# Probabilities transposed on VectorE in 32-row blocks, and V multiplied in eight tiles of 32 rows and 64 columns

## The chip, the cores and the metric

One core of a Trainium2 chip runs the whole kernel. The metric is the device time of one launch in microseconds. The kernel before was timed three times: 888.75, 889.93 and 890.03 us, median 889.93 us.

## What is computed

A block of two layers on x of 4 batches x 1024 tokens x 256 features, in fp32. The first is a gated cross attention to a short context (64 rows per batch, 16 heads of 64), the second a mixture of experts (8 experts, the best two per token, each 256 to 1024 to 256).

```python
qh = jnp.einsum('bld,hdk->hblk', q, w_qs)          # q = layernorm(x)
kh = jnp.einsum('bld,hdk->hblk', k, w_ks)          # k = v = context
vh = jnp.einsum('bld,hdk->hblk', v, w_vs)
attn = jax.nn.softmax(jnp.einsum('hblk,hbmk->hblm', qh, kh), axis=-1)
out = jnp.einsum('hblm,hbmk->hblk', attn, vh) * qh  # the output is gated by the query
...
x = x + jnp.tanh(g_xattn[0]) * (out @ w_proj.T + b_proj)
x = x + jnp.tanh(g_ffn[0]) * ffn(layernorm(x))      # 8 experts, top 2
```

## The kernel before, in words

The 4096 tokens are cut into eight groups g of 512, each of four tiles t of 128 (`T`, `G`, `NG`, lines 68 to 70). Two groups share a batch. The 16 heads are handled as eight pairs (`NP`), and the pairs as two halves of four: `halves` (L359) makes two buffers, `qT` and `aT` are each such a pair of buffers with features or context rows on the partitions and the 512 tokens of the group along them.

The main loop (L1109) runs g from 0 to 10 and t from 0 to 3. I call one g a stage. A stage does, for tile t of group g:

- `probabilities` (L381): eight score products per tile into the two-bank PSUM tile `sc` (pool `ps2`, two buffers, L100), then row maximum (L394), subtraction (L396) on VectorE, exponential on ScalarE (L399), row sum (L401) and reciprocal (L402) on VectorE, and the product with the reciprocal on GpSimd (L404). The result `pr` has tokens on the partitions.
- `transpose_probabilities` (L408), one tile behind: eight TensorE transposes (L414) into two PSUM banks `pa`, each copied by ScalarE into `aT` (L415).
- `queries` (L366) for the next group: per pair two products (L370) into a bank, copied by ScalarE (L377).
- `attend` (L419), for the group before, in four steps q at t = 1: per step two banks `po`, four products of 64 rows and 64 columns with 512 tokens streaming (L428), then two VectorE products (L437) that multiply the bank into `qT` in place. Between the steps stand the query products of the loop.
- `project` (L439), for the group before, at t = 2 and 3: 32 products (L445) per call, and one VectorE operation (L452) that adds the result to x.
- two groups behind: layernorm for the second layer (`ln_norm`, L266; transposes L281, copies L286), router logits (L467, copies L475 and L479), and every second stage `route` (L483) and `place` (L528).

`values` (L333) makes V in stage 0 and ScalarE copies it into `vs` in four pieces per bank (L352). All one-bank PSUM tiles, those of `pq`, `pa`, `po`, `pp`, `pt`, `pl`, come from one pool of four buffers, `ps1` (L101, `bank` L106). Large SBUF blocks come from three shared sets: "group" (8), "weight" (7) and "hidden" (2) (L93). The expert weights of the second layer take "weight" blocks as they come free. From stage 6 on, the experts' slots (`run_slots`, L994: gather, L899, L978, scatter) run between the attention's steps, and from about 440 us they are alone.

The text gives the order in which work is offered; the framework's scheduler then orders each engine's queue by priority and by what it takes to be ready, assigns the buffers and places the semaphores. Every engine works through its queue in that order. `keep_in_program_order` and `issue_after` pin a few instructions.

A hardware matmul record is half an fp32 product: every L370, L385, L428, L445 product appears as two MATMUL records, a transpose (L281, L414) as one.

Of the kernel before, what the change touches and what calls it, by code (L numbers as in the profile page):

```python
# [15 lines left out]
P = 128  # L16
# [5 lines left out]
def kernel(  # L22
# [14 lines left out]
    out: bass.AP,  # L37
):


# [81 lines left out]
    dram = ctx.enter_context(tc.tile_pool(name="dram", bufs=1, space=bass.MemoryType.DRAM))  # L122
    normed = dram.tile([N, D], F32, tag="normed", name="normed")
    lists = dram.tile([E * N + BEHIND, 2], I32, tag="lists", name="lists")
    outf = out.rearrange("b l d -> (b l) d")
# [64 lines left out]
    kT = [keys_of[b // 2][:, b % 2] for b in range(B)]  # L190
    vs = block([P, B, NP, DK], "vs", "weight")

# [140 lines left out]
    def values(ctxT):  # L333

        n = 512 // P
        for b0 in range(0, B, 2):
            for p0 in range(0, NP, n):
                pv = bank(f"pv_{b0}_{p0}")
                for c in range(NC):
                    nc.tensor.matmul(  # L340
                        pv,
                        ctxT[:, c, b0 * M : (b0 + 2) * M],
                        wv[:, c, p0 * P : (p0 + n) * P],
                        start=(c == 0),
                        stop=(c == NC - 1),
                    )
                pvv = pv.rearrange("p (q j r k) -> p q j r k", j=2, r=2, k=DK)
                q0 = p0 // 2
                for i in range(2):
                    to = vs[:, b0 + i].rearrange("p (q r) k -> p q r k", r=2)  # L350
                    for j in range(2):
                        nc.scalar.copy(  # L352
                            to[j * M : (j + 1) * M, q0 : q0 + n // 2],
                            pvv[i * M : (i + 1) * M, :, j],
                        )
                yield


    def halves(name, share="group"):  # L359

        return [block([P, NP // 2, G], f"{name}_{i}", share) for i in range(2)]

    def of_pair(t, p):
# [17 lines left out]
    def probabilities(g, t, qT):  # L381

        sc = ps2.tile([P, NP // 2, 2, 2, M], F32, tag="ps2", name=f"sc_{g}_{t}")
        for p in range(NP):
            nc.tensor.matmul(  # L385
                sc[:, p // 2, :, p % 2, :],
                of_pair(qT, p)[:, t * P : (t + 1) * P],
                kT[g // GB][:, p, :],
                start=True,
                stop=True,  # L390
            )
        scv = sc.rearrange("p q r j m -> p (q r j) m")
        mx = small.tile([P, H], F32, tag="mx", name=f"mx_{g}_{t}")
# [14 lines left out]
    def transpose_probabilities(g, t, pr, aT):  # L408
        prv = pr.rearrange("p (i j) m -> p i (j m)", j=2)
        n = 512 // P  # L410
        for p0 in range(0, NP, n):
            pt = bank(f"pa_{g}_{t}_{p0}")
            for i in range(n):
                nc.tensor.transpose(pt[:, i * P : (i + 1) * P], prv[:, p0 + i, :], ident)  # L414
            nc.scalar.copy(  # L415
                aT[p0 // n][:, :, t * P : (t + 1) * P], pt.rearrange("p (i q) -> p i q", i=n)
            )

    def attend(g, q, qT, aT):  # L419

        po = [bank(f"po_{g}_{2 * q + j}") for j in range(2)]
        for r in range(2):
            for j in range(2):
                half = slice(j * M, (j + 1) * M)
                i = q * 2 + r
                nc.tensor.matmul(  # L428
                    po[j][r * DK : (r + 1) * DK],
                    vs[half, g // GB, i, :],  # L430
                    of_pair(aT, i)[half],
                    start=True,
                    stop=True,
                )
        for j in range(2):
            own = of_pair(qT, 2 * q + j)
            nc.vector.tensor_tensor(own, po[j], own, ALU.mult)  # L437

# [670 lines left out]
    for g in range(NG + 3):  # L1109
        attention_ends = g >= NG  # L1110
        if g < NG:
            qT, aT = qTs[g], halves(f"aT_{g}", "hidden" if g % 2 and g + 1 < NG else "group")
            held[g] = (qT, aT)
# [4 lines left out]
        ends = before_last % GB == GB - 1 and before_last >= 0  # L1118
        for t in range(T):
            if g < NG:  # L1120
                pr = probabilities(g, t, qT)
# [4 lines left out]
            products = [(h, p) for h, pairs in parts[g].items() for p in pairs[t]]  # L1126
            if 0 < g <= NG and t == 1:
                for q in range(NP // 2):
                    attend(g - 1, q, *held[g - 1])
                    for h, p in products[q : q + 1]:  # L1130
                        queries(h, qTs[h], [p])
                products = products[NP // 2 :]
            for h, p in products:
# [4 lines left out]
            if g == 0:  # L1138
                for _ in range(value_parts[t]):
                    next(pending_values)  # L1140
            if 0 <= before_last < NG and t < 2:
                norm_again(before_last, t)
# [72 lines left out]
```

## Time and profile before

| what | value |
|---|---|
| median of three runs | 889.93 us |
| the profiled execution, its own time | 918.12 us |
| its span in the trace | 916.3 us |
| mean granted TensorE clock | 0.986 |
| TensorE busy (matmul) | 871.4 us, 95% of the span |
| VectorE busy | 327.8 us, 36% |
| ScalarE busy | 263.9 us, 29% |
| GpSimd busy | 403.0 us, 44% |
| L414 transposes of probabilities, x256 | 33.5 us busy |
| L428 products with V, x256 | 37.2 us busy |
| L437 VectorE products after them, x64 | 40.3 us busy |
| L415 ScalarE copies of transposes, x64 | 34.6 us busy |
| scores of tile 1 start in stages 1 to 7 | 74.9, 117.4, 164.0, 212.5, 260.2, 308.9, 351.0 us |

The profile gives, for one execution, each engine's busy time, the instructions by source line, what each one waited for and the chain of work that ended last. A busy time of matmuls is a union of records whose ends are modelled, so a TensorE that is 95% busy is not one at 95% of its peak; what counts is the distance from one start to the next. A mean in nanoseconds is the length of one record, which for matmuls overlaps its neighbours.

### The profile page before, as it was taken

The numbers are of one execution on the slowest core, as the hardware profiler recorded it, in microseconds if no ns is written. First come the engines' busy times: TensorE is split into PE (matmuls) and PEld (weight loads), VectorE is DVE, ScalarE is ACT, GpSimd is POOL, SyncE is SP. The second block draws the span as 40 slices with busy tenths as digits, with TensorE's granted clock in tenths as the row PEclk, the third lists the DMA queues.
The fourth block names the chain that finished last, engine by engine and source line by source line (L and its number), as shares of the span: only waits on it lengthen the run. The fifth ranks groups of instructions, "written<-read, shape, count | busy, mean of one in ns | idle before, by whom it ended". The sixth has DMA issues, their size and how long they took to land.

```text
span 916.3 us, 11723 instructions
## 1 busy us (share of the span) xinstructions
PE 871.4 (95%) x4328; PEld 657.5 (72%) x4328; DVE 327.8 (36%) x729; ACT 263.9 (29%) x414; POOL 403.0 (44%) x392
## 2 busy tenths in 40 slices
PE   8999999999999998997997899999999999999995
PEld 5556858574857576865885787777777777888884
DVE  3467585777468748631155300000000001100010
ACT  4653353425242425432140121211211211121110
POOL 2051212146213553065447565555455555564443
PEclk9999999999999999998998899999999999999998
DMA  9600000001010225276372575744444564457111
GB/s 203 195 1 1 24 24 24 24 19 30 1 46 1 47 90 188 72 141 143 115 262 63 143 248 166 237 149 140 148 140 142 176 198 148 135 188 267 51 36 42
DMA packets 85279, 102.33 MB, mean 112 GB/s; under 512 B 29366, under 2 KB 71740, under 8 KB 85216
## 3 DMA queue, kind: packets, MB, share of 16 engines
q1 hardware_dynamic: 62656, 66.96, 24.4%
q0 software_dynamic: 11600, 25.25, 8.8%
q10 hardware_dynamic: 10960, 9.31, 3.7%
q8 instruction: 36, 0.59, 0.3%
q14 instruction: 27, 0.22, 0.1%
HBM read 84.75 MB, written 17.33 MB: 111 GB/s over the span
## 4 chain that ended last, share of the span: by engine, by line
PE 80%; DVE 10%; another core or an unknown queue 3%; issue 3%; DMA 1%; POOL 1%; ACT 1%; POOLq 0%; ACTq 0%; DVEq 0%
PE py L978 23%; PE ph L899 22%; PE pp L445 11%; PE pq L370 10%; PE sc L385 5%; PE pa L414 2%; PE pt L867 2%; PE po L428 2%; DVE qT L437 1%; PE pk L317 1%; DVE sm L401 1%; DVE pr L396 1%; DVE mx L394 1%; PE pt_b L281 1%
## 5 line engine op out<-in xcount | busy, mean ns | idle before, releaser
L978 PE MATMUL py<-w,hT 128*128 128x256 f32 (+1 forms) x1168 | 238.3, 369 | 9.2 <-issue 8.7
L899 PE MATMUL ph<-xT,w 128*128 128x256 f32 (+2 forms) x896 | 233.8, 418 | 2.1 <-ACT xT L872 1.2
L978 PEld LDWEIGHTS py<-w,hT 128*128 128x128 f32 (+1 forms) x1168 | 199.8, 184 | 40.2 <-issue 14.0
L899 PEld LDWEIGHTS ph<-xT,w 128*128 128x128 f32 x896 | 170.0, 191 | 57.5 <-issue 1.6
L907 ACT ACTIVATE hT<-ph 128x1024 f32<-128x1024 f32 (+3 forms) x84 | 69.9, 835 | 370.6 <-PE ph L899 319.5
L966 DVE TENSOR_SCALAR x<-py,ids 128x256 f32<-128x256 f32 (+1 forms) x72 | 33.5, 465 | 381.9 <-PE py L978 348.3
L404 POOL TENSOR_TENSOR pr<-pr,sm 128x1024 f32<-128x1024 f32 x32 | 60.9, 1902 | 218.1 <-DVE sm L402 202.1
L370 PE MATMUL pq<-nT_a,wq 128*128 128x512 f32 x256 | 117.0, 597 | 0.4 <-issue 0.2
L445 PE MATMUL pp<-wp,qT 128*128 128x256 f32 x512 | 113.2, 379 | 0.0
L445 PEld LDWEIGHTS pp<-wp,qT 128*128 128x128 f32 x512 | 97.0, 190 | 18.2 <-issue 5.3
L922 POOL DMA_INDIRECT x<-out_dram,ids x68 | 69.3, 1018 | 81.7 <-DMA out_dram<-x,ids 61.9
L845 POOL DMA_INDIRECT x<-normed,ids x68 | 67.9, 999 | 53.4 <-DMA ids<-lists 34.3
L970 POOL TENSOR_TENSOR x<-x,x 128x256 f32<-128x256 f32 (+1 forms) x67 | 48.3, 721 | 90.5 <-DVE x L966 77.8
L370 PEld LDWEIGHTS pq<-nT_a,wq 128*128 128x128 f32 x256 | 45.9, 190 | 53.5 <-issue 47.6
L939 POOL DMA_INDIRECT out_dram<-x,ids x68 | 69.0, 1015 | 23.2 <-POOL x L970 18.0
L568 POOL DMA_INDIRECT lists<-entry,to_row x64 | 62.1, 971 | 20.5 <-issue 17.9
L385 PEld LDWEIGHTS sc<-keys,qT 128*128 128x128 f32 x512 | 62.9, 192 | 7.9 <-issue 7.5
L385 PE MATMUL sc<-keys,qT 128*128 128x128 f32 x512 | 67.4, 278 | 0.0
L415 ACT COPY aT<-pa 128x512 f32<-128x512 f32 x64 | 34.6, 590 | 91.2 <-PE pa L414 71.1
L394 DVE TENSOR_REDUCE mx<-sc 128x16 f32<-128x1024 f32 x32 | 39.0, 1220 | 29.5 <-PE sc L385 28.3
L401 DVE TENSOR_REDUCE sm<-pr 128x16 f32<-128x1024 f32 x32 | 38.9, 1215 | 20.9 <-ACT pr L399 20.9
L377 ACT COPY qT<-pq 128x512 f32<-128x512 f32 x64 | 35.7, 582 | 28.4 <-PE pq L370 28.4
(209 smaller groups left out, 624.8 us busy)
## 6 DMA issues: line engine op xcount, KB each, us to landing
w<-in_L_ffn_w_dram SPq DMA_DIRECT2D x56, 1024.0 KB
out_dram<-x ACTq DMA_DIRECT2D x8, 512.0 KB
normed<-keep_b ACTq DMA_DIRECT2D x8, 512.0 KB
x<-in_x_dram SPq DMA_DIRECT2D x7, 512.0 KB
x<-normed,ids POOLq DMA_INDIRECT x68
x<-out_dram,ids POOLq DMA_INDIRECT x68
out_dram<-x,ids POOLq DMA_INDIRECT x68
wq<-in_L_xattn_w_qs_dram SPq DMA_DIRECT2D x4, 256.0 KB
```

Source lines behind the costliest of these rows:

```text
L370: nc.tensor.matmul(pq, wq[:, c, p * P : (p + 1) * P], nT[g][:, c, :], start=(c == 0), stop=(c == NC - 1),)
L385: nc.tensor.matmul(sc[:, p // 2, :, p % 2, :], of_pair(qT, p)[:, t * P : (t + 1) * P], kT[g // GB][:, p, :], start=True, stop=True,)
L404: nc.gpsimd.tensor_tensor(pr, pr, sm.unsqueeze(2).to_broadcast([P, H, M]), ALU.mult).ins
L445: nc.tensor.matmul(pp[:, i, :], of_pair(qT, p)[:, t * P : (t + 1) * P], wp[:, p, :], start=(p == 0), stop=(p == NP - 1),)
L568: nc.gpsimd.indirect_dma_start(out=lists, out_offset=bass.IndirectOffsetOnAxis(ap=to_row[:, k, i : i + 1], axis=0), in_=entry[:, k, i, :], ...
L845: gather = nc.gpsimd.indirect_dma_start(out=xin[t][:n], out_offset=None, in_=normed[: tokens_of(s)], in_offset=bass.IndirectOffsetOnAxis(a ...
L899: nc.tensor.matmul(ph[:, i, :], a[:, c, f * P : (f + 1) * P], xT[:, c, :], start=(c == 0), stop=(c == NC - 1),)
L907: nc.scalar.activation(hT[f0 // per_tile][:, f1 : f1 + step, :], ph, AF.Silu)
L922: gather = nc.gpsimd.indirect_dma_start(out=acc[t][:r], out_offset=None, in_=outf[:n], in_offset=bass.IndirectOffsetOnAxis(ap=ids[:r, t, 0 ...
L939: put = nc.gpsimd.indirect_dma_start(out=outf[:n], out_offset=bass.IndirectOffsetOnAxis(ap=ids[:r, t, 0:1], axis=0), in_=acc[t][:r], in_of ...
L970: nc.gpsimd.tensor_tensor(acc[t][:r], acc[t][:r], y[t][:r], ALU.add)
L978: nc.tensor.matmul(py[t][rows], hT[f // per_tile][:, f % per_tile, t * P : t * P + r], b[:, f, columns], start=(f == 0), stop=(f == NF - 1),)
```

## The change

V is not copied into `vs` any more. One copy per bank brings it into a block `made`, two DMAs write it to DRAM, and `load_values` reads each batch's V back into a block of its own, with the 64 context rows cut into two halves of 32 and each half repeated on the four quarters of the partitions (eight DMAs per batch, on SyncE's queue). The score tile is laid out pair by pair. The probabilities are transposed by VectorE, in blocks of 32 by 32, two instructions per tile; the four token quarters of a tile so come to lie on the four quarters of the partitions. `attend` is called twice per group, for half the pairs at a time, at t = 1 and t = 2 and ahead of `probabilities` there. It takes all four banks of `ps1` at once, one for each token quarter, and runs 64 products of 32 rows and 64 columns with 128 tokens streaming, two accumulating into each place; then four VectorE products.

```diff
     def values(ctxT):
...
+        made = block([P, B // 2, H * DK], "values", "weight")
...
-                        nc.scalar.copy(
-                            to[j * M : (j + 1) * M, q0 : q0 + n // 2],
-                            pvv[i * M : (i + 1) * M, :, j],
-                        )
+                nc.scalar.copy(made[:, b0 // 2, p0 * P : (p0 + n) * P], pv)
                 yield
+            nc.sync.dma_start(v_dram[b0 * M : (b0 + 2) * M, :], made[:, b0 // 2])
+
+    def load_values(b):
+
+        v_of[b] = block([P, M // U, H, DK], f"v_{b}", "weight")
+        for m in range(M // U):
+            rows = v_dram[b * M + m * U : b * M + (m + 1) * U, :].rearrange("m (h k) -> m h k", k=DK)
+            for a in range(T):
+                nc.sync.dma_start(v_of[b][a * U : (a + 1) * U, m], rows)
...
+    def for_probabilities(name, share):
+
+        return [block([P, T, NP * M // U, U], f"{name}_{i}", share) for i in range(2)]
...
     def transpose_probabilities(g, t, pr, aT):
-        prv = pr.rearrange("p (i j) m -> p i (j m)", j=2)
-        n = 512 // P
-        for p0 in range(0, NP, n):
-            pt = bank(f"pa_{g}_{t}_{p0}")
-            for i in range(n):
-                nc.tensor.transpose(pt[:, i * P : (i + 1) * P], prv[:, p0 + i, :], ident)
-            nc.scalar.copy(
-                aT[p0 // n][:, :, t * P : (t + 1) * P], pt.rearrange("p (i q) -> p i q", i=n)
+
+        n = H * M // 2
+        for h in range(2):
+            nc.vector.transpose(
+                aT[h][:, t], pr.rearrange("p h m -> p (h m)")[:, h * n : (h + 1) * n].rearrange("p (b u) -> p b u", u=U)
             )
...
-    def attend(g, q, qT, aT):
...
-        po = [bank(f"po_{g}_{2 * q + j}") for j in range(2)]
-        for r in range(2):
-            for j in range(2):
...
+    def attend(g, h, qT, aT):
+
+
+        po = [bank(f"po_{g}_{h}_{a}") for a in range(T)]
+        for i in range(NP // 2):
+            for m in range(M // U):
+                for r in range(2):
+                    for a in range(T):
+                        quarter = slice(a * U, (a + 1) * U)
+                        nc.tensor.matmul(
+                            po[a][r * DK : (r + 1) * DK, i * T * U : (i + 1) * T * U],
+                            v_of[g // GB][quarter, m, h * NP + 2 * i + r, :],
+                            aT[h][quarter, :, (2 * i + r) * (M // U) + m, :],
+                            start=(m == 0),
+                            stop=(m == M // U - 1),
+                        )
+        own = qT[h].rearrange("p i (t a u) -> p a i t u", t=T, u=U)
+        for a in range(T):
+            nc.vector.tensor_tensor(
+                own[:, a], po[a].rearrange("p (i t u) -> p i t u", t=T, u=U), own[:, a], ALU.mult
+            )
...
         for t in range(T):
+            if 0 < g <= NG and t in (1, 2):
+                attend(g - 1, t - 1, *held[g - 1])
             if g < NG:
                 pr = probabilities(g, t, qT)
...
-            if 0 < g <= NG and t == 1:
-                for q in range(NP // 2):
-                    attend(g - 1, q, *held[g - 1])
-                    for h, p in products[q : q + 1]:
-                        queries(h, qTs[h], [p])
-                products = products[NP // 2 :]
...
+            if (g, t) == (0, T - 1):
+                load_values(0)
+                load_values(1)
+            elif g % GB == GB - 1 and g > GB - 1 and g // GB + 1 < B and t == 0:
+                load_values(g // GB + 1)
```

More of the change, by code (lines that the diff above doesn't have):

```diff
@@ L123 @@
     normed = dram.tile([N, D], F32, tag="normed", name="normed")
+    v_dram = dram.tile([B * M, H * DK], F32, tag="v", name="v_dram")
     lists = dram.tile([E * N + BEHIND, 2], I32, tag="lists", name="lists")
@@ L190 @@
     kT = [keys_of[b // 2][:, b % 2] for b in range(B)]
-    vs = block([P, B, NP, DK], "vs", "weight")
+    U = P // T
+    assert T == 4 and M % U == 0
+    v_of = {}
     ident = const.tile([P, P], F32, tag="ident", name="ident")
@@ L346, in values @@
                     )
[L347 to L350, printed above, removed]
-                    for j in range(2):
-                        nc.scalar.copy(
-                            to[j * M : (j + 1) * M, q0 : q0 + n // 2],
-                            pvv[i * M : (i + 1) * M, :, j],
-                        )
-                yield
+                nc.scalar.copy(made[:, b0 // 2, p0 * P : (p0 + n) * P], pv)
+                yield
+            nc.sync.dma_start(v_dram[b0 * M : (b0 + 2) * M, :], made[:, b0 // 2])
[5 more added lines that the diff above has]
+                nc.sync.dma_start(v_of[b][a * U : (a + 1) * U, m], rows)
     def halves(name, share="group"):
         return [block([P, NP // 2, G], f"{name}_{i}", share) for i in range(2)]
+    def for_probabilities(name, share):
+        return [block([P, T, NP * M // U, U], f"{name}_{i}", share) for i in range(2)]
     def of_pair(t, p):
@@ L381, in probabilities @@
     def probabilities(g, t, qT):
-        sc = ps2.tile([P, NP // 2, 2, 2, M], F32, tag="ps2", name=f"sc_{g}_{t}")
+        sc = ps2.tile([P, NP, 2 * M], F32, tag="ps2", name=f"sc_{g}_{t}")
         for p in range(NP):
             nc.tensor.matmul(
-                sc[:, p // 2, :, p % 2, :],
+                sc[:, p],
                 of_pair(qT, p)[:, t * P : (t + 1) * P],
@@ L391, in probabilities @@
             )
-        scv = sc.rearrange("p q r j m -> p (q r j) m")
+        scv = sc.rearrange("p q (r m) -> p (q r) m", m=M)
         mx = small.tile([P, H], F32, tag="mx", name=f"mx_{g}_{t}")
@@ L408, in transpose_probabilities @@
     def transpose_probabilities(g, t, pr, aT):
-        prv = pr.rearrange("p (i j) m -> p i (j m)", j=2)
-        n = 512 // P
-        for p0 in range(0, NP, n):
-            pt = bank(f"pa_{g}_{t}_{p0}")
-            for i in range(n):
-                nc.tensor.transpose(pt[:, i * P : (i + 1) * P], prv[:, p0 + i, :], ident)
-            nc.scalar.copy(
-                aT[p0 // n][:, :, t * P : (t + 1) * P], pt.rearrange("p (i q) -> p i q", i=n)
-            )
-    def attend(g, q, qT, aT):
-        po = [bank(f"po_{g}_{2 * q + j}") for j in range(2)]
-        for r in range(2):
[L425 to L437, printed above, removed]
+        n = H * M // 2
+        for h in range(2):
+            nc.vector.transpose(
+                aT[h][:, t], pr.rearrange("p h m -> p (h m)")[:, h * n : (h + 1) * n].rearrange("p (b u) -> p b u", u=U)
+            )
+    def attend(g, h, qT, aT):
[17 more added lines that the diff above has]
+            )
     def project(g, qT, t0):
@@ L1111 @@
         if g < NG:
-            qT, aT = qTs[g], halves(f"aT_{g}", "hidden" if g % 2 and g + 1 < NG else "group")
+            qT, aT = qTs[g], for_probabilities(f"aT_{g}", "hidden" if g % 2 and g + 1 < NG else "group")
             held[g] = (qT, aT)
@@ L1140 @@
                     next(pending_values)
+                if t == T - 1:
+                    for _ in pending_values:
+                        pass
+            if (g, t) == (0, T - 1):
[3 more added lines that the diff above has]
+                load_values(g // GB + 1)
             if 0 <= before_last < NG and t < 2:
```

## The prediction

> **What bounds the kernel now.** I read the busy rows in 40 slices first, then the instruction groups kept apart by shape, then the timeline of single stages.
>
> ```profile
> PE   8999999999999998997997899999999999999995
> ...
> DVE  3467585777468748631155300000000001100010
> ```
>
> TensorE is full in every slice: it is the bound. VectorE is 50 to 80% busy only up to slice 17 (about 390 us), the attention stages, where this change works.
>
> ```profile
> L428 PE MATMUL po<-aT,vs 64*64 64x512 f32 x256 | 37.2, 609 | 3.8 <-DVE qT L437 2.7 <-issue 0.9
> ...
> L414 PE MATMUL pa<-ident,pr 128*128 128x128 f32 x256 | 33.5, 274 | 1.1 <-POOL pr L404 1.1
> ...
> L978 PE MATMUL py<-w,hT 128*64 128x128 f32 x160 | 9.8, 276 | 0.0
> ```
>
> A record overlaps its neighbours, so I count start-to-start distances in the trace: 0.11 us for 128 streaming columns, 0.22 for 256, 0.43 for 512. L428's records start four abreast, within 0.02 us, the next four 0.43 later. L978's 64-column form runs two abreast (160 in 9.8 us: 0.12 a pair).
>
> Now the timeline, at two places where VectorE meets GpSimd and one where TensorE goes idle:
>
> ```profile
> 117.31 1.90 POOL L404 TENSOR_TENSOR pr<-pr,sm 128x1024 f32<-128x1024 f32 x1 [11.49 <-DVE sm L402]
> ...
> 117.43 1.93 DVE L277 TENSOR_SCALAR keep_b<-x,mv_b,rstd_b 128x256 f32<-128x256 f32 x1
> ```
> ```profile
> 421.83 1.34 PE L467 MATMUL pl<-nT_b,gw 128*32 128x128 f32 x16 [6.48 <-ACT nT_b L286]
> ```
> ```profile
> 414.00:422.00 8.00, 1.52 (x13) 1.07 (x15) 0.83 (x2) 0.71 (x2) 6.05 (x7) 0.82 0.89 134
> 422.00:426.00 4.00, 3.97 (x23) 2.52 (x20) 0.48 (x2) 0.46 (x1) 1.19 (x2) 0.50 0.43 168
> ```
>
> A `keep_b` that takes 0.33 us from start to start takes 1.93 when it falls beside the GpSimd product: it ends when that ends. And after TensorE stood for 6.48 us, its granted clock (third number from the end) was 0.50 until 426: 4.2 us of work at half speed, 2.1 us lost.
>
> **What the skill says.** "TensorEngine Tiling (Array Packing)", section Tiling Modes: 32x64 gives 8 independent tiles. The trace shows 4 (L428), not 8. The same page, Gotcha 1: different row tiles write to different PSUM banks; so four row tiles hold four banks, all of `ps1`. L428's two row tiles do use two. "TensorE: Matmul & The Clock Gate", Part 1: an idle window of about 3.4 us halves the clock. The trace agrees: 6.48 us did, gaps of 1.77 us at 190 and 286 us left it at 1.0. "VectorE: DVE Perf Modes", The three transpose paths: VectorE transposes 32x32 blocks only, 311 ns for 128x128 bf16. No run here shows one in fp32.
>
> **Part by part.**
>
> *Removed.* 256 transposes at 0.11: 28 us of TensorE, 3.5 per stage; and 64 ScalarE copies (0.59 each), beside TensorE's work, worth nothing by themselves. Also the waits of the old attention: stage 2, from tile 1's scores at 117.4 to the next stage's at 164.0, takes 46.5, and its products are 44.8 by the distances above, so 1.7 of waits. Stage 6 (308.9 to 351.0) loses 4.4 around L428, behind the early table's operations on VectorE; stages 3 and 5 about 3.4, of which 1.8 (a transpose waiting for `xn`) stays.
>
> *Products with V.* Before, per stage 16 products, 32 records of 512 columns four abreast: 8 x 0.43 = 3.4 us. After, 128 products, 256 records of 128 columns eight abreast: 32 x 0.11 = 3.5 us. Nothing gained, nothing lost, if eight run abreast. Bounds: never under 3.4 (same columns per tile); 7.0 if only four do. I take 3.5; the excess would mostly lie inside the waits below.
>
> *VectorE.* Eight transposes of 128x512 per stage. The page's 311 ns for 128 elements, less 128 at 0.96 GHz, leaves 0.18 fixed; 512 elements then come to 0.71 alone. L437, also 512 elements, is 0.676 alone and 0.62 in a row; I take 0.60, bounds 0.53 (an element per cycle and nothing else) and 1.2 (two passes for fp32). 4.8 us per stage onto 32 to 36 of 47: it still fits. The L437 products stay 64 at 0.62, in strips of 32.
>
> *V through DRAM.* Sixteen 128 KB reads for batches 0 and 1 are issued near 57 us, first needed near 75; 2 MB at the 200 GB/s of the first slices is 10 us. Later batches load a stage ahead on an SP queue that has nothing else until stage 6. From there V of two batches holds two "weight" blocks where `vs` held one, so one expert block comes later, but it is used 40 us on. Nought; cover gone, a few us once. The 16 copies L352 (5.9 us) become four.
>
> *The new waits.* The built order of the changed kernel shows what stands where. Stage 2, TensorE: attend half 0; scores of tile 1; two query products; transposes for the router; scores of tiles 2 and 3 with the router between; attend half 1; five products of the next stage's first scores; a query product; project. Each `attend` takes all four banks.
>
> (a) Entry, half 0: it needs the bank of the query product just before, which ScalarE copies: 0.2 + 0.58 + 0.05 = 0.85.
> (b) After half 0, the next query product waits for the first L437 product, queued behind `keep_b` and two transposes that need the GpSimd product (till 2.6 after the stage's start): multiplied by 5.95, TensorE there at 4.4. 1.5 in stages 2 and 4; 0 in 3 and 5, where no statistics stand before; 4.6 in 6 behind the early table (5.4 us).
> (c) Entry, half 1: the router's last bank, 0.95.
> (d) After half 1, the query product needs a bank that only the first L437 product frees, and VectorE's queue has that product behind all of this, in us from the end of tile 2's scores: maximum 1.35; reciprocal and router copy 1.75; subtraction 2.9; copy 3.1; two transposes, which wait until 3.6 for GpSimd, 4.8; sum 5.95; `xn`, reciprocal 6.5; `xn` 6.85; a third `xn`, held by GpSimd from 6.7 to 8.6 as at 117.43, 8.95; maximum 10.1; transpose, subtraction, transpose 12.45; L437 product 13.1; 13.2 with its semaphore. TensorE meanwhile: scores and router 2.5, wait (c) to 3.2, attend to 4.95, five products to 6.05. It stands 7.1 us. The same count gives 7.6 in stages 3 and 5 (routing's comparisons in the queue), 6.1 in stage 6, and 4.2 in stage 1, where four products, softmax and transposes stand between.
> (e) An idle 6 to 7 us contains a whole 3.4 us window nearly always: 2.1 of clock as measured at 422; four of stages 2 to 6.
>
> *Sum.* Stage 2 or 4: -3.5 - 1.7 + 0.85 + 1.5 + 0.95 + 7.1 = +5.2. Stage 3 or 5: -3.5 - 1.6 + 0.85 + 0.95 + 7.6 = +4.3. Stage 6: -3.5 - 4.4 + 0.85 + 4.6 + 0.95 + 6.1 = +4.6. Together 23.6, and 4 x 2.1 = 8.4 of clock. Stage 0: 24 transposes, -2.6. Stage 1: -3.5 - 1.1 + 0.85 + 0.8 + 4.2 = +1.3. Stage 7 (40 transposes; its second half waits 6.5 behind routing): -4.4 - 1.0 + 0.85 + 0.95 + 6.5 = +2.9. Stage 8, where VectorE is nearly idle: -2.5. Sum +31.1. All of it passes on: the router of the last group and every late slot follow the attention.
>
> The profiled execution is 918.1 (span 916.3), so it would be 949. The median of the plain runs is 28.2 lower; the trace's odd stretches (a 17.4 us link at 403.8 of the chain, "issue" gaps at 493 to 505) lie outside stages 1 to 7, so I add the same 31.1 to the median: 889.9 + 31.1 = 921.
>
> **Rivals.**
>
> A, *the removed TensorE work comes through.* If VectorE frees the banks in time, that is, the chain of 13.2 in (d) takes under 6.05, and (b) likewise: 28 us of transposes and some 12 of old waits go, entries (8 x 1.8 = 14) come: 889.9 - 26 = 864. For it: TensorE is the bound, VectorE idles a quarter of each stage. Against: that is a latency chain, with GpSimd's 1.9 in it twice. 0.08.
>
> B, *the same waits, without the clock and the GpSimd lock.* (d) shrinks by 1.75 in stages 2 to 5 and 7, and gaps of 5.4 may miss a window: 921 - 8.8 - 8.4 = 904. For it: the lock is seen at `keep_b` only beside L404's start. 0.22.
>
> C, *slow transposes or tiles not abreast.* At 1.2 us each the four in (d)'s chain add 2.4 per stage, 17 over seven; 938. 0.12.
>
> D, *no net change*: chains half as long as I count, removals and waits cancel: 890. 0.03.
>
> **How the numbers follow.** Main case 0.55 at 921, from 911 to 931; A 0.08, B 0.22, C 0.12, D 0.03. Range 898 to 940 leaves out A, D and a tail of C. A difference of under 0.2% a measurement of this kernel can't tell from none. Faster 0.09, same 0.03, slower 0.88.
>
> **What would show it.** In the changed profile: L414 and L415 gone, 64 transposes near 0.6 to 0.7 us; products with V starting eight within about 0.05 us, then 0.11 apart; query and project products with idle time ended by the L437 product, 4 to 8 us once per stage; clock dips to 0.5 after them; stages 2 to 6 at 50 to 54 us instead of 42 to 49; after 440 us as before. I am wrong if the stages shorten, if the waits end on something else, or if the stages from 440 us on change.

## The result, and the profile after

The changed kernel takes 938.43 us (median of four runs, 937.79 to 938.84) where the kernel before takes 889.64 us (888.75 to 890.03): 1.0549 times as long, interval 1.0531 to 1.0567, or 48.8 us more. The forecast was 921 us, 31 us more. The direction and the mechanism were right; the increase was short by 17.7 us. The result lies 1.6 us below the upper end of the stated range (898 to 940) and outside the main case's 911 to 931, so the range held with little to spare.

The profiled execution of the changed kernel is one of its plain runs (938.66 us, span 936.6 us). That of the kernel before had been 28 us longer than its plain runs, so one more was profiled (first experiment, span 887.6 us); every difference below is against that one. The two spans differ by 49.0 us.

The busy rows in 40 slices, and the granted clock in tenths:

```profile
PE   7996997979699896969999999999999999999995
DVE  3476685698738975584215800000000000100010
PEclk9999998989899898989999999999999999999998
```

TensorE was full in nearly every slice. Now it has a hole about every second slice up to slice 18 (about 420 us), and the clock dips with it. The second half of the kernel is as it was: from the router's last product, at 456.9 us before and 505.3 after, to the end it takes 430.7 and 431.3 us. The groups that answer to those shown of before (busy us, mean ns of a record, then the idle time just ahead and what ended most of it):

```profile
L381 PE MATMUL pq<-nT_a,wq 128*128 128x512 f32 x256 | 125.1, 632 | 37.5 <-DVE qT L444 37.5
...
L454 PE MATMUL pp<-wp,qT 128*128 128x256 f32 x512 | 118.3, 390 | 5.8 <-DVE qT L444 5.8
...
L435 PE MATMUL po<-aT,v 32*64 32x128 f32 x2048 | 49.3, 287 | 9.8 <-ACT qT L388 5.2
L422 DVE STREAM_TRANSPOSE aT<-pr 128x512 f32<-128x512 f32 x64 | 42.3, 689 | 35.3 <-POOL pr L414 35.2
```

L414 and L415 of before (transposes and their copies) are gone, L422 does their work on VectorE. The query product (L381; L370 before) stands 37.5 us and the project product (L454; L445 before) 5.8 us for the gating product on VectorE (L444; L437 before). In the kernel before the same two groups stand 0.4 and 0.0 us:

```profile
L370 PE MATMUL pq<-nT_a,wq 128*128 128x512 f32 x256 | 117.1, 597 | 0.4 <-ACT aT L415 0.4
L445 PE MATMUL pp<-wp,qT 128*128 128x256 f32 x512 | 113.2, 379 | 0.0
...
L428 PE MATMUL po<-aT,vs 64*64 64x512 f32 x256 | 36.1, 608 | 2.0 <-DVE qT L437 1.8
L414 PE MATMUL pa<-ident,pr 128*128 128x128 f32 x256 | 33.5, 274 | 1.1 <-POOL pr L404 1.1
```

One such wait, in stage 2 (start, length, engine, line; in brackets the idle time before it and what ended it):

```profile
140.08 1.38 PE L395 MATMUL sc<-keys,qT 128*128 128x128 f32 x10
...
141.57 2.27 DVE L282 TENSOR_SCALAR xn_a<-x,mv_a,rstd_a 128x256 f32<-128x256 f32 x2
141.80 1.90 POOL L414 TENSOR_TENSOR pr<-pr,sm 128x1024 f32<-128x1024 f32 x1 [3.07 <-DVE sm L412]
143.77 1.21 DVE L404 TENSOR_REDUCE mx<-sc 128x16 f32<-128x1024 f32 x1
144.90 0.69 DVE L422 STREAM_TRANSPOSE aT<-pr 128x512 f32<-128x512 f32 x1
145.53 1.18 DVE L406 TENSOR_TENSOR pr<-sc,mx 128x1024 f32<-128x1024 f32 x1
146.64 0.68 DVE L422 STREAM_TRANSPOSE aT<-pr 128x512 f32<-128x512 f32 x1
147.25 2.44 DVE L444 TENSOR_TENSOR qT<-po,qT 128x512 f32<-128x512 f32 x4
147.95 3.78 PE L381 MATMUL pq<-nT_a,wq 128*128 128x512 f32 x4 [6.49 <-DVE qT L444]
```

The products with V are over at 140.1 (the next scores start), and the four gating products could start then. They start at 147.25, because VectorE's queue has nine operations first: from the row sum at 139.99 to the transpose at 146.64. Two of them, the `xn` pair, take 2.27 us beside GpSimd's product; where GpSimd's product is cut short (third experiment) the same pair takes 0.65 us. TensorE gets five score products (10 records) in and then stands 6.49 us. The windows around it, with the granted clock third from the end:

```profile
144.00:148.00 4.00, 0.05 (x1) 0.05 (x1) 4.00 (x6) 1.06 (x1) 0.00 (x0) 0.71 0.60 152
148.00:152.00 4.00, 4.00 (x6) 1.85 (x7) 3.06 (x5) 0.23 (x1) 0.76 (x1) 0.50 0.00 0
```

In the second of them VectorE has let TensorE go, and TensorE works four microseconds at half clock. At that clock two query-product records start 0.85 us apart instead of 0.43.

To see where the 49 us arise I take one event per stage in both traces, the first of the 16 query-product records that stand in a row at the start of stages 2 to 6, then the last query products of stage 6, then the end. The forecast's own terms, summed over the same stretches (its 8.4 us of clock spread over stages 2 to 6), stand beside.

| stretch | before, us | after, us | more | forecast |
|---|---|---|---|---|
| to stage 2 (stages 0 and 1) | 110.4 | 115.7 | +5.3 | -1.3 |
| stage 2 | 46.6 | 53.5 | +6.9 | +6.9 |
| stage 3 | 48.6 | 52.3 | +3.7 | +6.0 |
| stage 4 | 46.7 | 56.2 | +9.5 | +6.9 |
| stage 5 | 48.6 | 52.5 | +3.9 | +6.0 |
| stage 6, to its last query products | 36.4 | 47.1 | +10.7 | +6.3 |
| from there to the end | 550.4 | 559.5 | +9.1 | +0.4 |

Of the first row, 2.3 us lie ahead of the first query products (17.4 against 15.1 us). In the changed kernel and its variants below, which don't differ there, that start lies between 15.6 and 17.4 us, so a difference of up to 2 us in the first row says nothing of the change.

### The profile page after: what moved, and what is told of

Read it like the earlier page. It is cut to its first block, busy times and chain, and to the rows that moved or that the text cites. A ratio compares the mean times of both kernels' runs of the same rounds, so it can differ in the third digit from the quotient of the medians.

```text
span 936.6 us, 14799 instructions
## 1 busy us (share of the span) xinstructions
PE 861.4 (92%) x5864; PEld 664.5 (71%) x5864; DVE 373.3 (40%) x793; ACT 224.5 (24%) x336; POOL 404.1 (43%) x392
## 4 chain that ended last, share of the span: by engine, by line
PE 71%; DVE 17%; ACT 3%; POOL 3%; issue 3%; DMA 2%; POOLq 0%; SPq 0%; ACTq 0%
PE py L987 23%; PE ph L908 22%; PE pp L454 12%; PE pq L381 7%; DVE mx L404 3%; DVE sm L411 2%; POOL pr L414 2%; DVE aT L422 2%; DVE pr L406 2%; DVE qT L444 2%; ACT pr L409 2%; PE pt L876 2%; PE sc L395 1%; DVE xn_a L282 1%; PE po L435 1%
## 5 line engine op out<-in xcount | busy, mean ns | idle before, releaser
L987 PE MATMUL py<-w,hT 128*128 128x256 f32 (+1 forms) x1168 | 232.6, 365 | 0.0
L381 PE MATMUL pq<-nT_a,wq 128*128 128x512 f32 x256 | 125.1, 632 | 37.5 <-DVE qT L444 37.5
L414 POOL TENSOR_TENSOR pr<-pr,sm 128x1024 f32<-128x1024 f32 x32 | 61.0, 1905 | 221.4 <-DVE sm L412 173.4
L454 PE MATMUL pp<-wp,qT 128*128 128x256 f32 x512 | 118.3, 390 | 5.8 <-DVE qT L444 5.8
L454 PEld LDWEIGHTS pp<-wp,qT 128*128 128x128 f32 x512 | 101.2, 198 | 28.0 <-issue 6.5
L381 PEld LDWEIGHTS pq<-nT_a,wq 128*128 128x128 f32 x256 | 48.5, 201 | 86.4 <-issue 46.0
L948 POOL DMA_INDIRECT out_dram<-x,ids x68 | 69.6, 1024 | 22.2 <-POOL x L979 17.7
L979 POOL TENSOR_TENSOR x<-x,x 128x256 f32<-128x256 f32 (+1 forms) x67 | 48.8, 728 | 60.8 <-DVE x L975 54.7
L577 POOL DMA_INDIRECT lists<-entry,to_row x64 | 62.4, 975 | 24.3 <-issue 15.6
L435 PE MATMUL po<-aT,v 32*64 32x128 f32 x2048 | 49.3, 287 | 9.8 <-ACT qT L388 5.2
L422 DVE STREAM_TRANSPOSE aT<-pr 128x512 f32<-128x512 f32 x64 | 42.3, 689 | 35.3 <-POOL pr L414 35.2
L435 PEld LDWEIGHTS po<-aT,v 32*64 32x64 f32 x2048 | 39.1, 134 | 22.4 <-ACT qT L388 9.5
```

The lines of the kernel that those rows point to most:

```text
L381: nc.tensor.matmul(pq, wq[:, c, p * P : (p + 1) * P], nT[g][:, c, :], start=(c == 0), stop=(c == NC - 1),)
L414: nc.gpsimd.tensor_tensor(pr, pr, sm.unsqueeze(2).to_broadcast([P, H, M]), ALU.mult).ins
L435: nc.tensor.matmul(po[a][r * DK : (r + 1) * DK, i * T * U : (i + 1) * T * U], v_of[g // GB][quarter, m, h * NP + 2 * i + r, :], aT[h][quar ...
L454: nc.tensor.matmul(pp[:, i, :], of_pair(qT, p)[:, t * P : (t + 1) * P], wp[:, p, :], start=(p == 0), stop=(p == NP - 1),)
L577: nc.gpsimd.indirect_dma_start(out=lists, out_offset=bass.IndirectOffsetOnAxis(ap=to_row[:, k, i : i + 1], axis=0), in_=entry[:, k, i, :], ...
L948: put = nc.gpsimd.indirect_dma_start(out=outf[:n], out_offset=bass.IndirectOffsetOnAxis(ap=ids[:r, t, 0:1], axis=0), in_=acc[t][:r], in_of ...
```

## Experiments

**The kernel before once more**, for a trace without the 28 us. No edit.

> The kernel before, unchanged, for a profile that is as long as its plain runs (the profiled execution shown before the prediction was 28 us longer). All theories: about 890 us, and up to the first product with V of stage 8 the same stages as before (405.9 us). If the 28 us lay outside stages 1 to 7, as the prediction took it, the stretch from there to the end is 482 us instead of 510; if not, the stages themselves are shorter here.

Measured: 889.33 us, span 887.6 us, clock 0.997. The stages start where they started in the first trace, within 1.3 us up to stage 6; the first product with V of stage 8 starts at 403.8 instead of 405.9 us, and from there to the end it takes 483.8 us where the first trace has 510.4. So 26.6 of the 28.7 us lay outside stages 1 to 7, as the forecast took it.

**The gating products ahead of the softmax.** Only VectorE's queue is changed.

```diff
-                attend(g - 1, t - 1, *held[g - 1])
-            if g < NG:
-                pr = probabilities(g, t, qT)
-            if last:
-                transpose_probabilities(*last)
+                gated = attend(g - 1, t - 1, *held[g - 1])
+            with tc.issue_after(gated) if 0 < g <= NG and t in (1, 2) else nullcontext():
+                if g < NG:
+                    pr = probabilities(g, t, qT)
+                if last:
+                    transpose_probabilities(*last)
```

> The changed kernel with one thing moved: in VectorE's queue the four gating products of a half (L444) stand ahead of the softmax of the tile whose scores come next and of the transposes after it, not behind them. Nothing is removed. Theory (the query product waits for a bank that the first gating product frees, and that product is queued behind some 7 us of softmax): the idle time of 6 to 7 us at L381 once per stage falls to about 1 us (end of the products with V, one gating product of 0.65, a semaphore), and the stretches at clock 0.5 behind it go; 6 stages x (5.6 + 1.7 to 2.1) + some 3 for stage 1 is about 47 us: 892, from 884 to 902. Rival 1 (the products with V take longer on TensorE, they don't run eight abreast): the gap was cover for work that comes anyway, no more than 2 us gained, 936 to 939. Rival 2 (VectorE is full, 64 transposes are too much for it): the wait moves to the softmax, the next stage's first half of attention waits instead, 925 to 938.

Measured: 921.7 us, 1.0362 (1.0319 to 1.0405) of before. The wait itself went as the theory said:

```profile
L381 PE MATMUL pq<-nT_a,wq 128*128 128x512 f32 x256 | 116.0, 595 | 4.0 <-DVE qT L444 4.0
L455 PE MATMUL pp<-wp,qT 128*128 128x256 f32 x512 | 115.7, 383 | 0.0
L435 PE MATMUL po<-aT,v 32*64 32x128 f32 x2048 | 47.7, 286 | 18.5 <-issue 8.1
```

From 43.3 us of idle time at the two product groups to 4.0, and the busy time of both falls by 11.7 us, as fewer dips of the clock fall on them. By the last query products this kernel is 30 us ahead of the changed one (347.1 against 377.1 us), 1.8 of them from an earlier start. But the total gain is only 17 us, between the ranges of the theory and of rival 2. Two things take the rest: TensorE stalls inside the products with V (18.5 us ahead of L435 instead of 9.8, 5 of them in one half of stage 4), and behind the last query products 10 us are lost. There scores wait 6.2 us up to 366.2: VectorE stood 6.9 us ahead of two transposes, for a product of GpSimd's that came behind six gathers of the experts (351.1 to 358.7). The router's rows wait 3.7 us for VectorE's comparisons, which stand behind gating products and softmax. So rival 1 falls, the theory holds for the wait, and rival 2 holds for a part: moving one late operation forward makes the next one late.

**GpSimd's division cut to one column of 64.** Nearly all of the normalisation is left out.

```diff
-            nc.gpsimd.tensor_tensor(pr, pr, sm.unsqueeze(2).to_broadcast([P, H, M]), ALU.mult).ins
+            nc.gpsimd.tensor_tensor(pr[:, :, 0:1], pr[:, :, 0:1], sm.unsqueeze(2), ALU.mult).ins
```

> The changed kernel, but GpSimd divides only one column per head by the row sum (16 of 1024 elements), so nearly all of the normalisation is left out; its place in the queues and its dependences stay. Theory: the chain ahead of the gating product loses the time in which VectorE waits for GpSimd's product or is held by it, about 0.7 + 1.6 us in the second half of each stage and 1.6 in the first half of stages 2 and 4: 938 - 7 x 2.3 - 3 = 919, and down to 908 if some of the gaps then leave the clock at 1.0. Rival (VectorE's own work is the chain, GpSimd plays no part): 934 to 938.

Measured: 924.7 us, 1.0379 (1.0339 to 1.0419).

```profile
L381 PE MATMUL pq<-nT_a,wq 128*128 128x512 f32 x256 | 125.1, 632 | 22.6 <-DVE qT L444 22.6
```

The four long waits of stages 2 to 5 fall from 6.49, 6.02, 6.97 and 6.45 us to 4.05, 4.18, 3.96 and 4.17: 1.8 to 3.0 less, 2.4 in the mean, where 2.3 were expected. By the last query products 20.7 us are gained; 7 to 8 are lost again afterwards, where a router's transpose at 434 us stands 6.1 us. The total lies between the theory's 919 and the rival's 934. GpSimd's part in the chain is shown; it is about a third of the wait.

**The kernel before without its transposes.** What V multiplies is then not the reference's.

```diff
-            pt = bank(f"pa_{g}_{t}_{p0}")
-            for i in range(n):
-                nc.tensor.transpose(pt[:, i * P : (i + 1) * P], prv[:, p0 + i, :], ident)
-            nc.scalar.copy(
-                aT[p0 // n][:, :, t * P : (t + 1) * P], pt.rearrange("p (i q) -> p i q", i=n)
-            )
+            nc.scalar.copy(aT[p0 // n][:, :, t * P : (t + 1) * P], prv[:, p0 : p0 + n, :])
```

> The kernel before with its 256 TensorE transposes of the probabilities left out: ScalarE copies the probabilities untransposed into aT, so what V multiplies is not the reference's. Theory (TensorE is the bound in the attention stages, and each transpose costs its 0.11 us there): 890 - 28 = 862, and 3 to 6 us less if waits go with them: 856 to 864. Rival (the transposes lie beside other waits, and the removal is worth less than its own time): 870 to 888.

Measured: 898.1 us. The total can't be used: other values route other tokens, and one more expert slot runs (928 records of L894 instead of 896). The stages ahead of the slots can. The stages 2 to 5 last 44.8, 46.7, 44.8 and 46.7 us, 1.9 less each, where the 32 transposes were priced at 3.5. The last query products start at 321.9 instead of 337.2 us: 15.3 us for about 208 transposes, where 0.11 each makes 22.9. The rest reappears beside the products with V:

```profile
L423 PE MATMUL po<-aT,vs 64*64 64x512 f32 x256 | 42.7, 611 | 4.8 <-DVE qT L432 2.8
```

42.7 us busy and 4.8 idle instead of 36.1 and 2.0. The rival was right for these stages: about a third of the transposes' time is not gained. That it had lain in waits of the attention that come anyway is read from this line alone; the copies that take the transposes' place on ScalarE were not varied.

**TensorE kept at work while it waits.** Useless products of 512 columns into the first bank, which the products with V overwrite.

```diff
         po = [bank(f"po_{g}_{h}_{a}") for a in range(T)]
+        for i in range(5 * h):
+            nc.tensor.matmul(po[0], wq[:, 0, :P], nT[g][:, 0, :], start=True, stop=True)
```

> The changed kernel with useless TensorE work put into its idle stretch: five whole query-like products of 512 columns (10 records x 0.43 = 4.3 us) into the first bank, ahead of the second half's products with V, which then overwrite them. Theory (in the second half TensorE waits for VectorE's queue, and the idle 6 to 7 us also halve the clock for 6.8 us, seven times): the gating products end where they ended, the idle time falls to some 2 us, no stretch at 0.5 follows, and the kernel gains the clock's share, about 15 us, less what shows where the wait was short: 926, from 920 to 934. Rival 1 (the dips of the clock cost nothing, something else follows in their place): 937 to 941. Rival 2 (TensorE's own work sets the time there): seven times 4.3 us more, 960 to 970.

Measured: 980.1 us, 1.1007 (1.0967 to 1.1047), beyond every expectation. The trace shows why. VectorE's queue in stage 2:

```profile
147.34 1.22 DVE L411 TENSOR_REDUCE sm<-pr 128x16 f32<-128x1024 f32 x1 [0.57 <-ACT pr L409]
...
148.99 1.90 POOL L414 TENSOR_TENSOR pr<-pr,sm 128x1024 f32<-128x1024 f32 x1 [5.84 <-DVE sm L412]
150.92 1.30 DVE L422 STREAM_TRANSPOSE aT<-pr 128x512 f32<-128x512 f32 x2 [2.08 <-POOL pr L414]
152.15 2.44 DVE L446 TENSOR_TENSOR qT<-po,qT 128x512 f32<-128x512 f32 x4
152.86 2.08 PE L381 MATMUL pq<-nT_a,wq 128*128 128x512 f32 x2 [8.45 <-DVE qT L446]
```

The scheduler put the row sum, the reciprocal and the two transposes of tile 3 ahead of the gating products as well, presumably since it expects the products with V later now. TensorE worked 4.3 us more and still stood 8.45 us. The run doesn't separate what it was made for; it shows that the gating product's place in VectorE's queue sets the time.

**The same with VectorE's order held.** The edit above, and:

```diff
+        with tc.issue_after(gated) if g and t == 3 else nullcontext():
             nc.vector.tensor_reduce(sm, pr, AX.X, ALU.add)
...
+        with tc.issue_after(gated) if name in ("1", "3") else nullcontext():
             nc.vector.tensor_reduce(rank, ahead, AX.X, ALU.add)
```

and the same for the subtraction and the transposes at t = 3 of stages 3 and 5.

> The same useless products as in the run that came out at 980 us (4.3 us of 512-column products ahead of the second half's products with V), but with VectorE's queue held in the order of the changed kernel: row sum of tile 3, and in stages 3 and 5 also its subtraction, tile 2's transposes and the router's ranks, stay behind the gating products, which in the 980 us run they had overtaken. Theory (the gating product's place in VectorE's queue sets when TensorE goes on; the clock's dips cost about 15 us on top): TensorE's idle time at L381 falls to 1 to 3 us per stage, few dips follow, 925, from 917 to 934. Rival 1 (the useless work itself made the 980): 968 to 982 again. Rival 2 (dips cost nothing): 936 to 942.

Measured: 940.9 us, 1.0554 (1.0518 to 1.0591).

```profile
140.33 2.10 PE L440 MATMUL po<-aT,v 32*64 32x128 f32 x128
...
145.81 2.44 DVE L449 TENSOR_TENSOR qT<-po,qT 128x512 f32<-128x512 f32 x4
146.50 2.42 PE L381 MATMUL pq<-nT_a,wq 128*128 128x512 f32 x3 [2.99 <-DVE qT L449]
```

26 us of added TensorE work (six halves, 60 records at 0.43) cost 1.4 us up to the last query products: they start at 377.0 us, in the changed kernel at 377.1, and this run began 1.5 us earlier. In stage 2 the query product comes 32.28 us after the stage's event, without the added work 32.29; in stages 3, 5 and 6 the two are within 0.5 us. In stage 4 it comes 5.1 us later: a router's product waits 4.1 us there, and the half stops for 2.5 us. So rival 1 falls: but for that stage, the gating product sets when TensorE goes on, with or without 4.3 us more of TensorE's work before it. The clock's share did not come: the dips were not avoided, only made shorter (eight of 30.7 us together instead of seven of 47.8), and TensorE worked through nearly all of their time, 29.9 us against 31.0. Where none followed, in stage 5, the stretch from the query product to the next stage's event is 19.90 us instead of 21.15. That speaks for a price of about 1.3 us for a dip there. But the total lies in rival 2's range and not in the theory's; rival 2 is weakened, not settled.

**Query products in other banks.**

```diff
-            pq = bank(f"pq_{g}_{p}")
+            pq = bank(f"pq_{g}_{p}", spare)
...
-                queries(h, qTs[h], [p])
+                queries(h, qTs[h], [p], g > 0 and t >= 2)
```

> The changed kernel, but the query products offered at t = 2 and 3 of stages 1 to 7 take a bank of the two-bank pool of the scores, so that they wait for no bank of the attention. VectorE's queue still has the gating products behind softmax and transposes. Theory (what is late is the gating product in VectorE's queue; banks only say who notices first): the query product doesn't wait any more, the project product behind it waits for the gated queries instead, 5 to 8 us once per stage ended by L444: 938, from 930 to 946. Rival (four banks held at once are the trouble): the idle time goes, 7 x 5.5 us and the clock, 890 to 903.

Measured: 944.0 us, 1.0582 (1.0537 to 1.0627).

```profile
L454 PE MATMUL pp<-wp,qT 128*128 128x256 f32 x512 | 126.2, 406 | 33.3 <-DVE qT L444 33.3
L381 PE MATMUL pq<-nT_a,wq 128*128 128x512 f32 x256 | 117.6, 600 | 1.2 <-DVE qT L444 1.2
```

The wait changed its place, from the query product to the project product, which reads what the gating product writes. So the rival falls. The forecast named the bank as what TensorE waits for; that was the first thing it met, and what is late is the gating product.

**Half the columns per product with V.** Half of the tokens stay ungated.

```diff
-                            po[a][r * DK : (r + 1) * DK, i * T * U : (i + 1) * T * U],
+                            po[a][r * DK : (r + 1) * DK, i * T * U : i * T * U + 2 * U],
...
-                            aT[h][quarter, :, (2 * i + r) * (M // U) + m, :],
+                            aT[h][quarter, :2, (2 * i + r) * (M // U) + m, :],
```

> The changed kernel with each product with V over 64 of its 128 columns: as many instructions, half the columns; half of the tokens stay ungated and unattended. Read from it: first to last start of one half, 2.3 to 2.5 us in the changed kernel where nothing stalls it, where 16 waves of eight at 0.11 would take 1.75. If the columns set it (eight abreast, but slower waves), it falls to 1.2 to 1.4 us; if the 256 records and their 256 weight loads set it, some 19 ns a record, it stays at 2.2 to 2.5.

Measured (910.0 us, one run): a first half that doesn't stall takes 1.95 to 2.05 us from first to last start instead of 2.52, the second half of stage 2 takes 1.62 instead of 2.40. Neither expectation fits. The two runs with useless work explain it. There the second halves that nothing holds up take 1.83 us: 128 records in 16 waves of eight, 0.115 us a wave. Eight records of the first wave start within 0.05 us. So eight tiles do run abreast, at the rate that the forecast took. With half the columns a wave still takes about 0.09 us once it runs, so below 128 columns something else sets the pace, probably the number of records; no run here separates the two. The 2.52 us of a first half contain a stop of 0.56 us behind the first eight weight loads (122.81 to 123.37 us in stage 2, ended by ScalarE's copy): the wait for the last of the four banks, which the forecast counts as (a).

**VectorE's order changed twice.** The gating products ahead of the softmax in stages 1 to 6, and up to stage 5 a tile's two transposes behind maximum and subtraction of the next tile, but for the places that the condition names.

```diff
+    GF = 6
...
+            with tc.issue_after(gated) if 0 < g <= GF and t in (1, 2) else nullcontext():
                 if g < NG:
                     pr = probabilities(g, t, qT)
             if last:
-                transpose_probabilities(*last)
+                with nullcontext() if g > 5 or (g > 2 and (g % 2, t) in ((1, 3), (0, 0))) else tc.issue_after(lessened[0]):
+                    transpose_probabilities(*last)
```

> The changed kernel with VectorE's queue in another order and nothing else: in stages 1 to 6 the gating products of a half ahead of the next tile's softmax, as before, and up to stage 5 the two transposes of a tile behind maximum and subtraction of the next one, where GpSimd's product for them has ended. Theory (the place of the operations in VectorE's queue is what costs, not their number): against the first of the two orders alone, 921.7, the first attention's wait of 3.8 us and its clock (1.7) go, and the 10 us lost after the last query product, where the gating products held up softmax and routing: 905, from 898 to 914; what stays is the products' own excess, the router's waits and stages 6 to 8. Rival (VectorE has too much to do, an order only shifts the wait): 918 to 930.

Measured: 912.9 us, 1.0231 (1.0192 to 1.027), at the edge of what the theory gave. An order alone takes 25.5 us of the 48.8 away. Up to the last query products the lead is larger still: in the profiled execution, the slowest of the four (918.4 us), they start at 340.5 us, 36.6 ahead of the changed kernel, and 16.5 us are lost behind them, with waits of 4.5, 4.7, 3.7 and 7.7 us there. So what the run with the gating products ahead lost there did not come back, though these products stand in their old place from stage 7 on.

**The second of the two orders alone.** The same with `GF = 0`; `lessened` is the subtraction of the tile whose scores came last.

> The changed kernel with only the second of the two orders: up to stage 5 VectorE's two transposes of a tile behind maximum and subtraction of the next tile; the gating products where the scheduler puts them, behind the softmax. Theory: the first attention's wait (3.8 us of idle and 1.7 of clock at 73 us) goes, because the exponential, and the copies of the query products behind it in ScalarE's queue, no longer wait for GpSimd through VectorE; the idle time at L381 stays, shorter by the 0.7 to 1.2 us for which the transposes waited for GpSimd: 926, from 920 to 932. Rival (the first attention waits for V, which comes back from DRAM): the stall at 73 us stays, 932 to 938.

Measured: 926.9 us, 1.0421 (1.0386 to 1.0456): the theory's number. The stop in the first attention is gone (its first half takes 2.52 us from first to last start). In the changed kernel it was this:

```profile
71.44 1.30 DVE L422 STREAM_TRANSPOSE aT<-pr 128x512 f32<-128x512 f32 x2 [2.08 <-POOL pr L414]
...
75.21 1.06 ACT L409 ACTIVATE pr<-pr 128x1024 f32<-128x1024 f32 x1 [5.37 <-DVE pr L406]
76.17 1.05 ACT L388 COPY qT<-pq 128x512 f32<-128x512 f32 x2
...
76.79 4.07 PE L435 MATMUL po<-aT,v 32*64 32x128 f32 x124 [3.78 <-ACT qT L388]
```

V was back from DRAM by then: the last read of this stretch is issued by 67.0 us, and those whose landing the trace has take 2.5 to 5.3 us. TensorE waits for a bank that ScalarE's copy frees; the copy stands behind an exponential, that behind VectorE's subtraction, that behind two transposes, and those wait for GpSimd. Four queues, one behind the other.

**List writes of stage 4 moved away** (the order of 912.9 us as base), and **those of stage 8 too**.

```diff
-            elif g >= GB + 2 and before_last % GB == 0 and t < 2:
-                entries(before_last - 1, t + 1)
+            elif g >= GB + 2 and before_last % GB == 0 and late <= t < late + 2:
+                entries(before_last - 1, t - late + 1)
```

with `late` 2 in stage 4 (first run) or in stages 4 and 8 (second run), else 0.

> The changed kernel in the VectorE order that ran at 912.9 us, with one move: in stage 4 the two groups of list writes of the routing (GpSimd's indirect DMAs, L580) are offered at t = 2 and 3 instead of 0 and 1, so that they don't run beside the first half's products with V. There that run had a stall of 4.4 us in the middle of the products, with an instruction fetch of TensorE's queue under way (207.1 us). Theory (TensorE runs out of instructions in the 256 short ones of a half when its fetch falls among many small writes): the first half of stage 4 takes 2.5 us from first to last start instead of 11, with the clock whole after it: 905, from 900 to 909. Rival (the stall belongs to the place, to the statistics or the half itself): stays, 910 to 917.

> As the run with the list writes of stage 4 moved, and those of stage 8 moved in the same way; in the 912.9 us run TensorE stood for 7.7 us among four transposes there (425.0 to 432.7 us), with an instruction fetch at 424.5 beside list writes. Theory: that stall shrinks too, 898, from 892 to 906. Rival (in stage 8 the writes only meet another fetch): no gain over that run within 3 us.

Measured: 907.0 us, 1.0188 (1.0163 to 1.0213), and 907.7 us, 1.0184 (1.0126 to 1.0243). The first number lies where the theory had it, but the stall didn't go:

```profile
202.57 2.55 PE L437 MATMUL po<-aT,v 32*64 32x128 f32 x95
206.97 0.30 PE L437 MATMUL po<-aT,v 32*64 32x128 f32 x1 [1.85 <-issue]
207.24 0.37 ACTq L295 DMA_DIRECT2D normed<-keep_b  x1
209.21 0.74 PE L437 MATMUL po<-aT,v 32*64 32x128 f32 x4 [1.94 <-issue]
```

This half still takes 8.4 us from first to last start (7.5 in the second run). The packets of the last list write ahead of it end at 203.4, so they are not the cause. TensorE stops at 205.1 after 95 records, the trace's DMA records show a fetch of 16 KB in an instruction queue at 206.1, and a write of 512 KB follows at 208. The queue is most likely TensorE's: it has 48 fetches in the changed kernel and 36 in the one before, and TensorE's 3072 added records (1536 products, 1536 weight loads) are by far the largest difference. That it runs out of instructions fits, but is argued, not shown. The runs of the two versions overlap (909.6 to 918.4 against 905.4 to 914.4), so the gain of 5.9 us is not clear of their spread. The second run gained nothing more: the rival.

No version beat the kernel before. The best, 907 us, is 1.9% slower than it.

## Why the prediction was right, and where its size was off

*The new waits* was right in its mechanism: idle time ended by the gating product once per stage, seven times (3.4, 6.5, 6.0, 7.0, 6.5, 6.7, 5.8 us), clock dips behind it, the chain behind tile 2's scores with GpSimd in it. The full stages came to 52 to 56 us, where 50 to 54 had been named. Moving the gating product removed it, delaying it made it longer, other banks only moved it. In (d) the sum was 46.2 us, the trace has 41.8; in (b) 8.4, the trace has under 3. These were too high by some 10 us, and that hid a part of the terms that were too low: that the range held, 1.6 us below its end, owes as much to errors that cancel as to the sum.

The terms that were mis-sized the other way:

- *(a), the entry of a half*: for later stages 0.85 was right (in stage 2, from the end of the query product at 122.5 to the next scores at 125.3, 2.8 us pass, where 0.85 + 1.75 were taken). In the first attention it was 3.8 of idle and 1.7 of clock. The forecast looked at ScalarE's copy and not at what stands in ScalarE's queue ahead of it. That is some 3 us, and the clock; with the 2.3 us of the start it makes up the table's first row.
- *(e), the clock*: four dips of 2.1 us, 8.4, were taken. There are seven in stages 1 to 7, 47.8 us long together. TensorE worked through 31.0 us of them, so at half the pace up to 15.5 us are lost, 7 more. Stages 1 and 7 and one of stages 2 to 6 had been left out, and a dip outlasts the wait that starts it. The one stage that shows a price (stage 5, above) gives 1.3 us where this count gives 2.1, so the 7 is an upper bound.
- *Products with V*: eight abreast, 0.115 us a wave, as taken. Not foreseen is that some halves stop in their middle: 4.2, 4.0, 5.7, 4.5 and 3.3 us from first to last start in stages 4, 6, 7 and 8, where 2.5 are usual; 9 us together. For 2.2 of them in stage 7 the trace names ScalarE's evictions for the experts, and for a part of those in stages 6 and 8 operations for the routing and the experts on VectorE (0.7 and 0.2) and ScalarE (0.6); the rest, with nearly all of stage 4's, has no cause in it. With the dip behind stage 7's wait (2.3) and a transpose that waits 1.3, six of these nine make up the last row of the table.
- *Removed*: 28 us of transposes and 13.1 of old waits were taken off whole. Without the transposes the kernel before gains 15.3 us where 22.9 were priced, and its trace has 5.1 us of idle time at the three groups whose waits were to go (L414, L428, and L281's 2.0). The forecast had counted waits as a stage's length less its products; the idle columns would have shown fewer. The two overlap; about 7 us is what the sum leaves for them (2.3 of the start + 3 + 7 + 9 - 10 + 7 = 18), so this share is a remainder and was not measured by itself. Up to 2.5 of it is stage 8: the forecast took 2.5 us off there and gave no working for it, and from the first product with V of that stage to the router's last product it takes 56.2 us instead of 53.1.

*VectorE*: 0.60 us a transpose was taken, 0.689 is a record, 0.62 start to start in a row (144.90 alone, 138.77 two in 1.31). *V through DRAM* was nought, as taken: no group waits for it. Rival A failed since the chain in (d) never came under TensorE's own work; rival B because the dips and GpSimd's hold are both there; rival C's time, 938, was met without its cause, as transposes are fast and tiles are abreast.

The Trainium skill was right on the tiles: "TensorEngine Tiling (Array Packing)", Tiling Modes, has eight of 32x64, and eight run in 0.115 us a wave. On the clock it covers a part: "TensorE: Matmul & The Clock Gate", Part 1, says that an idle window of about 3.4 us halves the clock. Every dip of these traces, but the one at each end, lasts 3.4, 6.8, 10.2, 13.7 or 20.5 us, which fits such a window, and a wait of 3.37 us at 89.3 left the clock whole. But the window need not be idle: a wait of 2.99 us in the run with VectorE's order held was followed by a dip, and in the run with the gating products ahead the dip at 323.7 us follows 3.4 us in which TensorE was busy for 1.5 and no wait was longer than 1.0. So here the measurement decides: several short waits among the small products were followed by a dip too.

## What to carry to other kernels

Work taken from the engine that bounds and put on another is worth its time only where the second engine's queue doesn't answer back: list what stands ahead of the operation that gives back a bank or an operand, in that engine's queue and in each queue that this one waits for. An operation's place in a queue can cost more than its length: here another order took 25 of 49 us away. And take no removed work at its full time before you know that it didn't lie in a wait.

## What was not expected of the hardware

- The scheduler's order is part of an experiment: 4.3 us of TensorE work per stage moved four VectorE operations (in stage 2) and cost 42 us; with the order held it cost 2.5.
- Halves with 256 short instructions (128 matmul records and their weight loads) stop in their middle in stages 4 and 6 of most variants, for 1 to 8 us, with most of the idle time labelled "issue" and, in the stage 4 stops of the changed kernel and of the runs with another order, an instruction fetch beside the stop. The kernel before, with 32 records of products with V per stage instead of 256, has no stop of this kind. What sets it stays open.
- VectorE's transpose of 128x512 fp32 takes 0.69 us, about what its product of two 128x512 operands takes (2.44 to 2.48 us for four).
